# A graph network layer: 45 of its 1,563 row gathers replaced by column copies on chip, one more group of early x rows, and the node updates placed one group earlier

## The chip, the cores and the metric

The kernel runs on one core of one Trainium2 chip. A core has a matrix engine (PE, with its weight loads shown apart as PEld), a vector engine (DVE), a scalar engine (ACT), GpSimd (POOL) and a sync engine (SP) that here only issues transfers. Each engine takes its own instructions in program order and waits for the others through semaphores. The metric is the device time of one execution in microseconds (us), as the median of several runs.

## What is computed

There are 12,500 nodes with 64 features `x` and 200,000 edges with 32 features. An edge has a source and a destination; edges come sorted by destination. Every edge gives a message, messages are summed over the edges of a destination, a second small network updates the node, and the result is added to `x` and normalised over the 64 features:

```python
msg_in = concat([x[src], x[dst], edge_attr], axis=-1)        # 160 wide
messages = relu(msg_in @ mW1 + mb1) @ mW2 + mb2              # 160 -> 128 -> 64
aggregated = segment_sum(messages, dst, num_segments=12500)
upd = relu(concat([x, aggregated], axis=-1) @ uW1 + ub1) @ uW2 + ub2
out = layernorm(x + upd)
```

All data are float32.

## The kernel before

**Tables and tiles.** The first layer is linear before its relu, so the kernel computes two tables first: A = x @ (rows of `mW1` for the source) and B = x @ (rows for the destination) + `mb1`, each 12,500 x 128, both kept in device memory. Edges are worked in tiles of 128. A "group" `s` of this text is 8 tiles (`SUB`), a super group `g` is 16 tiles (`SUP`), so two groups make one super group. There are 1,563 tiles, 196 groups (the last has 3 tiles) and 98 super groups. Because the edges are sorted, the 128 destinations of a tile fall in a window of 32 nodes.

**One group.** For each group, `gather` (L147) has POOL issue one indirect transfer for each tile (L158), which brings the 128 rows of A that the sources name to one buffer of the pool `rows`. That pool has 6 buffers (`ROWB`); `frees` tells which group must be done before a buffer can be filled again. `edge_part` (L234) multiplies on PE the edge features, and a selection by destination, with a combined right side `rhs` (edge weights and the 32 window rows of B, loaded by SP in `windows`, L206), into a PSUM tile `pc`. `node_part` (L247) adds the gathered rows on DVE (L263), and ACT applies the relu (L264) into `h`. `collect` (L267) multiplies `h` on PE with a selection matrix (L276) to sum over edges by destination, into `ph`, and `aggregate` (L279) has DVE add each tile's 32 columns to `comb` (L288). The place in `comb` is read into registers first (L283), as the window's place is only known at run time.

**comb.** This is one tile of 128 partitions and two halves. Half 0 collects the hidden sums. Half 1 holds counts of edges in its first partition and, in partitions 64 to 127, the transposed `x`: column n is the feature vector of node n. `xload` brings it before the loop. `aggregate` adds to both halves at once, and what it adds in partitions 64 to 127 of half 1 is zero.

**The first groups.** While the tables are being computed (`chunk_a` on PE, ACT and DVE for A, `chunk_b` for B), the first `XG` = 7 groups don't gather from A but straight from `x`; `transpose` and a matmul in `node_part` (L257) then do the first layer for them.

**Node updates.** When the edges have moved past about 384 nodes, `columns` (L292) copies these columns of `x` to `xw` on ACT (L297), `update` and `residual` do the second network on PE (L304, L305, L315, L316) with a relu on ACT (L307), and `norm` finishes on DVE and stores the result. There are 54 such updates. Their places grow denser: from super group 62 on there is one in each super group, that is in every second group, because destinations are unevenly spread.

**Order.** The order is written out by hand in one loop over `s`, and each engine executes its part in that order: the gathers that may be issued, `norm` of an update, `windows`, `node_part(s)`, `columns`, `collect(s - 1)` and `aggregate(s - 1)`, `select` (DVE, L183 to L189), `load` and `counts` (ACT, L197) for the next super group in even groups, a part of table B in the early groups, `edge_part(s + 1)`, `update`, `residual`, and `rest`, which holds setting-up work at a few values of `s` (at group 10 it prepares the update's weights and checks the assumption about the windows). Waits between engines are set by the tiles that the instructions read and write. A tile counts as touched wherever the column is only known at run time, so everything that reads `comb` is ordered against every `aggregate`.

Of the kernel before, what the change touches and what calls it, by code (L numbers as in the profile page):

```python
# [10 lines left out]
F32 = mybir.dt.float32  # L11
I32 = mybir.dt.int32
AF = mybir.ActivationFunctionType
ALU = mybir.AluOpType
AX = mybir.AxisListType
ET = mybir.EngineType

P = 128
# [6 lines left out]
SUB = 8  # L25
# [9 lines left out]
PADWIN = 1000000  # L35
EK, SK = 0, DE
ROWB = 6
XG = 7
NCH = 8
HB = NCH // 2  # L40
EARLY = NCH * P
GE = 20
BS = 8
UB = 3
NCOL = (-(-N // P) + UB) * P
ONE = D - 1
# [15 lines left out]


@with_exitstack
def gnn_kernel(ctx: ExitStack, tc: tile.TileContext, x1T, x, eT, e_rows, src, dst, dst_row, wrow, wnext, whalf,
               mW1, mb1, mW2, mb2, uW1, ub1, uW2, ub2, out):

# [28 lines left out]

    src_s = const.tile([P, NT], I32, name="src_s")
    wint = const.tile([1, NTP], I32, name="wint")  # L100
    win0 = const.tile([1, GE * SUP], I32, name="win0")
    w1b = const.tile([P, DH], F32, name="w1b")
    b1 = const.tile([P, DH], F32, name="b1")

# [22 lines left out]
    cps = cpool.tile([P, WIN + SUP], F32, name="cps")  # L127
    slot = cps[:, :WIN]
    drc = const.tile([P, NT], F32, name="drc")
    flag_i = const.tile([1, 1], I32, name="flag_i")  # L130
    usup = const.tile([1, K], I32, name="usup")
    wh = const.tile([P, NTP // 2], I32, name="wh")
# [2 lines left out]

    rows = ctx.enter_context(tc.tile_pool(name="rows", bufs=ROWB))
    xg = {}

    def frees(s):

# [3 lines left out]
    def tiles(s):  # L144
        return range(s * SUB, min((s + 1) * SUB, NT))

    def gather(s):  # L147

        if s >= XG or s % 2 == 0:
            buf = rows.tile([P, SUB, DH], F32, name="xg")  # L150
        else:
            buf = xg[s - 1][0]
        d = DH if s >= XG else D
        a = buf.rearrange("p k (b d) -> p (k b) d", d=d)
        if s < XG:
            a = a[:, s % 2 * SUB:(s % 2 + 1) * SUB, :]
        for i, t in enumerate(tiles(s)):
            nc.gpsimd.indirect_dma_start(  # L158
                out=a[:, i, :], out_offset=None, in_=A[:, :] if s >= XG else x[:, :],
                in_offset=bass.IndirectOffsetOnAxis(ap=src_s[:, t:t + 1], axis=0))  # L160
        xg[s] = buf, a

    with tc.tile_pool(name="sup", bufs=2) as sup, tc.tile_pool(name="work", bufs=2) as work, tc.manual_schedule():
# [42 lines left out]
        def windows(g):  # L206

            nt = min(SUP, NT - g * SUP)
            r = rhs[g % 2]
            w, tab, n = (win0, B0, EARLY - WIN + 1) if g < GE else (wint, B, N)  # L210
            _, ws = nc.values_load_multi_w_load_instructions(
                w[0:1, g * SUP:g * SUP + nt], engines=[ET.SP], min_val=0, max_val=n - 1,
                skip_runtime_bounds_check_because="destinations are node numbers")
            for i in range(nt):
                q = SK + 64 * (i % 2)
                nc.sync.dma_start(r[q:q + WIN, i // 2, :], tab[bass.ds(ws[i], WIN), :])
# [17 lines left out]
        def edge_part(s):  # L234

            n = len(tiles(s))
            g, j = divmod(s, SUP // SUB)
            pc = psum.tile([P, 2, SUB // 2, DH], F32, name="pc")
            for i in range(n):
                k, b = divmod(i, 2)  # L240
                q, m = 64 * b, j * SUB // 2 + k

                nc.tensor.matmul(pc[:, b, k, :], L[g][q:q + 64, m, :], rhs[g % 2][q:q + 64, m, :],  # L243
                                 start=s >= XG or k == 0, stop=s >= XG)
            pcs[s] = pc

        def node_part(s):  # L247

            n = len(tiles(s))
            pc = pcs.pop(s)  # L250
            h = work.tile([P, 2, SUB // 2, DH], F32, name="h")
            if s < XG:
                xt = xs.pop(s)
                for i in range(n):
                    k, b = divmod(i, 2)
                    q = 64 * b
                    nc.tensor.matmul(pc[:, b, k, :], xt[q:q + 64, k, :], w1a[q:q + 64], start=False,  # L257
                                     stop=i + 2 >= n)
                nc.scalar.activation(h, pc, AF.Relu)
            else:  # L260
                a = xg.pop(s)[1].rearrange("p (k b) f -> p b k f", b=2)
                for b, m in parts(n):
                    nc.vector.tensor_tensor(h[:, b, m], pc[:, b, m], a[:, b, m], op=ALU.add)  # L263
                    nc.scalar.activation(h[:, b, m], h[:, b, m], AF.Relu)  # L264
            hs[s] = h

        def collect(s):  # L267
# [11 lines left out]
        def aggregate(s):  # L279

            n = len(tiles(s))
            ph = pht.pop(s)
            _, ws = nc.values_load_multi_w_load_instructions(  # L283
                wint[0:1, s * SUB:s * SUB + n], engines=[ET.DVE], min_val=0, max_val=N - 1,
                skip_runtime_bounds_check_because="destinations are node numbers")
            for i in range(n):
                to = comb[:, :, bass.ds(ws[i], WIN)]
                nc.vector.tensor_tensor(to, to, ph[:, i], op=ALU.add)  # L288

        us = {}  # L290

# [137 lines left out]
        for r in rhs:  # L429
            for o in (EK, EK + 64):  # L430
                nc.sync.dma_start(r[o:o + DE], mW1[2 * D:, :].unsqueeze(1).broadcast_to([DE, SUP // 2, DH]))
        relative(0, 8 * SUP)
        nc.vector.tensor_scalar(win0, wint[:, :GE * SUP], float(EARLY - WIN), None, op0=ALU.min)
        Q = NCOL // 4
        for k, c in enumerate(range(0, NB, NCH)):
            chunk_a(c)
            if k == 0:
                chunk_b(0, [B0v, Bv])
                windows(0)
            if k < 8:  # L440
                nc.vector.memset(comb[:P if k < 4 else ONE, k // 4, k % 4 * Q:(k % 4 + 1) * Q], 0.0)
            if k == 9:
                select(0)
                load(0)
                counts(0)
                for c in range(0, NCOL, XCH):
                    xload(c)
        columns_of(NCH, nc.sync)

        def rest(s):  # L450

            if s == 1:
                relative(8 * SUP, 8 * SUP + WCH)
            elif s == 2:
                relative(8 * SUP + WCH, NT)
                halves(4 * SUP, NTP // 2)
            elif s == BS:
                nc.sync.dma_start(wa, wrow.rearrange("o (p c) -> (o p) c", c=SUP))
                nc.sync.dma_start(wb, wnext.rearrange("o (p c) -> (o p) c", c=SUP))
                nc.scalar.dma_start(w2, mW2)  # L460
                nc.scalar.dma_start(u1a, uW1[D:2 * D, :])
                nc.scalar.dma_start(b2c, mb2.rearrange("(f o) -> f o", o=1))
                nc.vector.memset(uz[:D], 0.0)
                nc.vector.memset(ux[:D], 0.0)
                nc.vector.memset(eps, EPS)
                nc.vector.memset(ones, 1.0)
                nc.vector.memset(usup[:, 0:1], 0)
                nc.vector.tensor_copy(ux[D:], ident[D:, D:])
                nc.scalar.dma_start(uz[D:], uW1[0:D, :])
                nc.scalar.dma_start(ux[ONE:ONE + 1], ub2.rearrange("(o f) -> o f", o=1))  # L470
                nc.scalar.dma_start(ub1_s, ub1.rearrange("(f o) -> f o", o=1))
                nc.scalar.dma_start(u2, uW2)
            elif s == BS + 2:
                weights()
                checks()
# [14 lines left out]
        def checks():  # L490
# [30 lines left out]
            gap = work.tile([1, K + 1], F32, name="gap", bufs=1)  # L521
            nc.vector.tensor_tensor(gap[:, :K], uf[:, 1:], uf[:, :-1], op=ALU.subtract)
            nc.vector.tensor_scalar(gap[:, :K], gap[:, :K], float(UB * P - WIN), None, op0=ALU.is_gt)
            nc.vector.tensor_scalar(gap[:, K:], wint[:, GE * SUP - 1:GE * SUP], float(EARLY - WIN), None, op0=ALU.is_gt)
            bad = work.tile([1, 1], F32, name="bad", bufs=1)
            nc.vector.tensor_reduce(bad, gap, AX.X, ALU.add)
            nc.vector.tensor_tensor(flag_i, pf, bad, op=ALU.add)

        due = {SUP // SUB * (UPD[u + 1] if u + 1 < K else NSUP) + 1: u for u in range(K)}
        last = SUP // SUB * NSUP + 1
        transpose(0)
        edge_part(0)
        gathered = XG
# [1 line left out]
        for s in range(last + 3):  # L537
# [7 lines left out]
                windows(g + 1)  # L545
            if s < NSUB:
                node_part(s)
            if s in due and s < last:
                columns(due[s])
            if 1 <= s <= NSUB:  # L550
                collect(s - 1)
                aggregate(s - 1)
            if j == 0 and g + 1 < NSUP:
                select(g + 1)
                load(g + 1)
                counts(g + 1)
            if j == 1 and g + 2 < NSUP:
                loadd(g + 2)
            if chunks and s >= BS and chunks[0] < NCH + NB * (s + 1 - BS) / (SUP // SUB * (GE - 1) - BS):
                if len(chunks) > 1:  # L560
                    columns_of(chunks[1], nc.sync)
                chunk_b(chunks.pop(0), [Bv])
            if s + 1 < NSUB:
                if s + 1 < XG:
                    transpose(s + 1)
                edge_part(s + 1)
            if s == NSUB:
                columns(K - 1)
            if s in due:
                update(due[s], "pt" if s == last else "pu")  # L570
            if s - 1 in due:
# [168 lines left out]
```

## Time and profile before

| what | value |
|---|---|
| median of 3 runs | 1991.58 us (1988.15 to 1992.86) |
| time of the profiled execution | 1995.25 us |
| its span, first to last instruction | 1993.5 us |
| mean granted PE clock | 0.559 of full |
| DMA traffic | 211.74 MB, mean 106 GB/s |
| issued transfers of A rows (L158) | 1,507, and 56 of x rows |

The profile has several views. The page gives the busy time of each engine and the chain of work that ended last, followed back from the last instruction. The groups of instructions give busy time and the mean of one. The view of waits says which engine waited, at which line, for whom. The timeline gives single instructions with their start. "Issue" is idle time of an engine for which the profile shows nothing that it waits for. A name such as `xg<-tab_a,src_s` is what an instruction writes and what it reads; a `q` behind an engine's name is its sequencer, which handles register and semaphore instructions.

### The profile page before, as it was taken

The numbers are of one execution on the slowest core, as the hardware profiler recorded it, in microseconds if no ns is written. First come the engines' busy times: TensorE is split into PE (matmuls) and PEld (weight loads), VectorE is DVE, ScalarE is ACT, GpSimd is POOL, SyncE is SP. The second block draws the span as 40 slices with busy tenths as digits, with TensorE's granted clock in tenths as the row PEclk, the third lists the DMA queues.
The fourth block names the chain that finished last, engine by engine and source line by source line (L and its number), as shares of the span: only waits on it lengthen the run. The fifth ranks groups of instructions, "written<-read, shape, count | busy, mean of one in ns | idle before, by whom it ended". The sixth has DMA issues, their size and how long they took to land.

```text
span 1993.5 us, 31593 instructions
## 1 busy us (share of the span) xinstructions
PE 1364.8 (68%) x7851; PEld 1211.9 (61%) x7851; DVE 908.7 (46%) x2661; ACT 348.4 (17%) x479; POOL 1477.0 (74%) x1572
## 2 busy tenths in 40 slices
PE   3678876656566666566667766676686776776867
PEld 3577875556555666556566665665575655665756
DVE  5347544434343444444444444444454545454544
ACT  1121111111111111111111111121212121212111
POOL 7577777777777777777777777777777777777773
PEclk7665555555555555555555555556555656565555
DMA  8745554433333333333333333334333333333331
GB/s 219 217 118 151 158 139 117 115 88 100 88 99 89 99 91 99 91 97 92 99 91 94 97 100 91 97 96 102 95 99 97 96 100 98 98 98 98 98 98 39
DMA packets 244401, 211.74 MB, mean 106 GB/s; under 512 B 80542, under 2 KB 209022, under 8 KB 243824
## 3 DMA queue, kind: packets, MB, share of 16 engines
q0 software_dynamic: 50016, 100.70, 20.4%
q1 hardware_dynamic: 178644, 98.69, 17.9%
q10 hardware_dynamic: 15554, 10.31, 1.8%
q8 instruction: 63, 1.03, 0.2%
q14 instruction: 124, 1.02, 0.2%
HBM read 190.78 MB, written 18.68 MB: 105 GB/s over the span
## 4 chain that ended last, share of the span: by engine, by line
POOL 53%; issue 25%; PE 9%; DMA 8%; DVE 3%; SPq 1%; ACT 1%; DVEq 0%; ACTq 0%; POOLq 0%
POOL xg L158 53%; DMA xg<-tab_a,src_s 5%; PE ph L276 3%; DMA xl<-in_x1T 2%; PE pc L243 2%; DVE comb L288 2%; PE pu L304 1%; PE py L315 1%; DVE h L263 1%; PE pb L381 1%; PE pu L305 1%; PE py L316 1%; DMA l<-in_eT 0%; PE ph L274 0%; DVE o L333 0%
## 5 line engine op out<-in xcount | busy, mean ns | idle before, releaser
L158 POOL DMA_INDIRECT xg<-tab_a,src_s x1507 | 1423.0, 944 | 470.0 <-issue 444.2
L276 PEld LDWEIGHTS ph<-sel,h 128*128 128x128 f32 x3126 | 610.2, 299 | 34.4 <-issue 34.4
L276 PE MATMUL ph<-sel,h 128*128 128x32 f32 x3126 | 601.0, 363 | 0.0
L263 DVE TENSOR_TENSOR h<-pc,xg 128x1024 f32<-128x1024 f32 (+1 forms) x190 | 230.8, 1215 | 770.4 <-DMA xg<-tab_a,src_s 720.7
L243 PE MATMUL pc<-rhs,l 64*128 64x128 f32 x3126 | 408.9, 415 | 62.8 <-DMA l<-in_eT 24.5
L288 DVE TENSOR_TENSOR comb<-comb,ph 128x64 f32 x1563 | 345.6, 221 | 202.1 <-ACT xw L297 83.0
L243 PEld LDWEIGHTS pc<-rhs,l 64*128 64x128 f32 x3126 | 352.7, 303 | 82.8 <-DVE rs L330 30.3
L264 ACT ACTIVATE h<-h 128x1024 f32<-128x1024 f32 (+1 forms) x190 | 199.2, 1049 | 915.0 <-DVE h L263 881.7
L304 PE MATMUL pu<-comb,w2u 128*128 x108 | 88.9, 927 | 255.9 <-DVE comb L288 255.9
L274 PE MATMUL ph<-selb,one 128*128 128x256 bf16 x196 | 75.4, 384 | 239.7 <-DVE comb L288 156.8
L274 PEld LDWEIGHTS <-one 128*128 128x128 bf16 x196 | 27.3, 139 | 272.2 <-DVE comb L288 252.8
L304 PEld LDWEIGHTS pu<-comb,w2u 128*128 128x128 f32 x108 | 27.1, 312 | 271.3 <-DVE comb L288 271.3
L185 DVE TENSOR_TENSOR l<-l,cps 128x1024 f32<-128x1024 int32 (+1 forms) x101 | 123.3, 1221 | 4.8 <-DMA l<-in_dst_row 1.3
L197 ACT CAST selb<-sel 128x512 bf16<-128x512 f32 x98 | 60.4, 616 | 329.3 <-DVE sel L189 308.7
L315 PE MATMUL py<-ux,xw 128*128 128x64 f32 x324 | 87.0, 362 | 0.7 <-ACT hTu L307 0.7
L316 PE MATMUL py<-u,hTu 128*128 128x64 f32 x324 | 84.3, 354 | 0.0
L305 PE MATMUL pu<-xw,uz 128*128 128x384 f32 x108 | 80.1, 846 | 0.0
L307 ACT ACTIVATE hTu<-pu,ub_s 128x384 f32<-128x384 f32 x54 | 31.3, 580 | 270.7 <-PE pu L305 270.7
L315 PEld LDWEIGHTS py<-ux,xw 128*128 128x128 f32 x324 | 68.9, 263 | 10.8 <-issue 6.3
L316 PEld LDWEIGHTS py<-u,hTu 128*128 128x128 f32 x324 | 70.3, 268 | 0.0
L189 DVE TENSOR_TENSOR sel<-cps,drc 128x512 f32<-128x512 f32 x98 | 66.8, 682 | 0.1
L158 POOL DMA_INDIRECT xg<-in_x,src_s x56 | 53.0, 946 | 18.4 <-issue 16.5
(73 smaller groups left out, 420.2 us busy)
## 6 DMA issues: line engine op xcount, KB each, us to landing
l<-in_dst_row SPq DMA_DIRECT2D x196, 128.0 KB
l<-in_eT SPq DMA_DIRECT2D x196, 128.0 KB
rhs<-tab_b SPq DMA_DIRECT2D x1563, 16.0 KB
xg<-tab_a,src_s POOLq DMA_INDIRECT x1507
tab_b<-tb SPq DMA_DIRECT2D x13, 512.0 KB
tab_a<-tb ACTq DMA_DIRECT2D x12, 512.0 KB
out<-o SPq DMA_DIRECT2D x54, 96.0 KB
comb<-in_x1T SPq DMA_DIRECT2D x6, 520.0 KB
```

The lines of the kernel that those rows point to most:

```text
L158: nc.gpsimd.indirect_dma_start(out=a[:, i, :], out_offset=None, in_=A[:, :] if s >= XG else x[:, :], in_offset=bass.IndirectOffsetOnAxis(a ...
L185: nc.vector.tensor_tensor(l[r], l[r].bitcast(I32), node[r].unsqueeze(2).broadcast_to([r.stop - r.start, SUP // 2, P]), op=ALU.is_equal)
L243: nc.tensor.matmul(pc[:, b, k, :], L[g][q:q + 64, m, :], rhs[g % 2][q:q + 64, m, :], start=s >= XG or k == 0, stop=s >= XG)
L263: nc.vector.tensor_tensor(h[:, b, m], pc[:, b, m], a[:, b, m], op=ALU.add)
L264: nc.scalar.activation(h[:, b, m], h[:, b, m], AF.Relu)
L274: nc.tensor.matmul(ph[:, :n, 1, :], one0, SB[g][:, k0:k0 + n, :], start=True, stop=True)
L276: nc.tensor.matmul(ph[:, i, 0, :], h[:, i % 2, i // 2, :], S[g][:, k0 + i, :], start=True, stop=True)
L288: nc.vector.tensor_tensor(to, to, ph[:, i], op=ALU.add)
L304: nc.tensor.matmul(pu, w2u, comb[:, 0, bass.ds(n0, UB * P)], start=True, stop=False)
L305: nc.tensor.matmul(pu, uz, xw, start=False, stop=True)
L315: nc.tensor.matmul(py[:, i], xw[:, i * P:(i + 1) * P], ux, start=True, stop=False)
L316: nc.tensor.matmul(py[:, i], hT[:, i * P:(i + 1) * P], u2, start=False, stop=True)
```

## The change

Three things are changed.

1. In groups 15, 19, 23 and so on to 191 (one of four groups, 45 in all) the eighth tile is not gathered. Its 128 source columns are copied one by one from half 1 of `comb` to a tile `xo` of 128 columns (two such tiles take turns), and one more matmul in `edge_part` multiplies that tile with the source weights and adds it in `pc`. The copies of one tile are spread over the four iterations that come five to two groups ahead of it: in each, ACT copies 24 columns and DVE 8. The numbers of the columns are read to registers from a small table `srow`. DVE copies by adding a column of zeros that lies in PSUM. In such a group DVE's addition and ACT's relu are split, because the eighth tile has nothing to be added.
2. The first eight groups, not seven, are gathered from `x`. In the set-up the clipped copy of the windows' numbers is replaced by clipping in place, and two steps are moved: the first `windows` comes two chunks later, and the first `relative` four chunks later.
3. `columns`, `update`, `residual` and `norm` of each update come one group earlier, and `columns` stands behind `aggregate(s - 1)` in its iteration instead of ahead of it. The loop is one iteration shorter.

```diff
-XG = 7
+XG = 8
...
+CG = 4
+CF = 3 * CG
+CA = 24
+NCT = -(-(NSUB - CF) // CG)
...
+    srow = const.tile([NCT, P], I32, name="srow")
+    xo = [const.tile([P, P], F32, name=f"xo{k}") for k in range(2)]
...
+    def copied(s):
+        return s >= CF and s % CG == CG - 1 and len(tiles(s)) == SUB
...
-        for i, t in enumerate(tiles(s)):
+        for i, t in enumerate(tiles(s)[:SUB - copied(s)]):
             nc.gpsimd.indirect_dma_start(
...
+                c = copied(s) and i == n - 1
                 nc.tensor.matmul(pc[:, b, k, :], L[g][q:q + 64, m, :], rhs[g % 2][q:q + 64, m, :],
-                                 start=s >= XG or k == 0, stop=s >= XG)
+                                 start=s >= XG or k == 0, stop=s >= XG and not c)
+                if c:
+                    nc.tensor.matmul(pc[:, b, k, :], xo[s // CG % 2][q:q + 64], w1a[q:q + 64], start=False, stop=True)
...
-                for b, m in parts(n):
+                for b, m in parts(n - copied(s)):
                     nc.vector.tensor_tensor(h[:, b, m], pc[:, b, m], a[:, b, m], op=ALU.add)
                     nc.scalar.activation(h[:, b, m], h[:, b, m], AF.Relu)
+                if copied(s):
+                    nc.scalar.activation(h[:, 1, SUB // 2 - 1], pc[:, 1, SUB // 2 - 1], AF.Relu)
...
+        def copies(s):
+            t = (s + 2) // CG * CG + CG - 1
+            if t < CF or not t < NSUB or not copied(t):
+                return
+            n = P // CG
+            k = (s + 2) % CG * n
+            r = t // CG - CF // CG
+            to = xo[t // CG % 2]
+            for a, b, e, copy in ((k, k + CA, ET.Activation, nc.scalar.copy),
+                                  (k + CA, k + n, ET.DVE, lambda o, i: nc.vector.tensor_tensor(o, i, slot[D:, 0:1], op=ALU.add))):
+                _, v = nc.values_load_multi_w_load_instructions(
+                    srow[r:r + 1, a:b], engines=[e], min_val=0, max_val=N - 1,
+                    skip_runtime_bounds_check_because="sources are node numbers")
+                for i in range(a, b):
+                    copy(to[D:, i:i + 1], comb[D:, 1, bass.ds(v[i - a], 1)])
...
-        relative(0, 8 * SUP)
-        nc.vector.tensor_scalar(win0, wint[:, :GE * SUP], float(EARLY - WIN), None, op0=ALU.min)
         for k, c in enumerate(range(0, NB, NCH)):
             chunk_a(c)
             if k == 0:
                 chunk_b(0, [B0v, Bv])
+            if k == 2:
+                w0 = wint[:, :GE * SUP]
+                nc.vector.tensor_scalar(past, w0[:, GE * SUP - 1:], float(EARLY - WIN), None, op0=ALU.is_gt)
+                nc.vector.tensor_scalar(w0, w0, float(EARLY - WIN), None, op0=ALU.min)
                 windows(0)
+            if k == 4:
+                relative(0, 8 * SUP)
...
-        due = {SUP // SUB * (UPD[u + 1] if u + 1 < K else NSUP) + 1: u for u in range(K)}
-        last = SUP // SUB * NSUP + 1
+        due = {SUP // SUB * (UPD[u + 1] if u + 1 < K else NSUP): u for u in range(K)}
+        last = SUP // SUB * NSUP
...
-            if s in due and s < last:
-                columns(due[s])
             if 1 <= s <= NSUB:
                 collect(s - 1)
                 aggregate(s - 1)
+            if s in due:
+                columns(due[s])
...
                 chunk_b(chunks.pop(0), [Bv])
+            copies(s)
             if s + 1 < NSUB:
...
-            if s == NSUB:
-                columns(K - 1)
             if s in due:
                 update(due[s], "pt" if s == last else "pu")
```

More of the change, by code (lines that the diff above doesn't have):

```diff
@@ L64, in gnn_kernel @@
 @with_exitstack
-def gnn_kernel(ctx: ExitStack, tc: tile.TileContext, x1T, x, eT, e_rows, src, dst, dst_row, wrow, wnext, whalf,
+def gnn_kernel(ctx: ExitStack, tc: tile.TileContext, x1T, x, eT, e_rows, src, src_row, dst, dst_row, wrow, wnext, whalf,
                mW1, mb1, mW2, mb2, uW1, ub1, uW2, ub2, out):
@@ L100, in gnn_kernel @@
     wint = const.tile([1, NTP], I32, name="wint")
-    win0 = const.tile([1, GE * SUP], I32, name="win0")
+    past = const.tile([1, 1], F32, name="past")
     w1b = const.tile([P, DH], F32, name="w1b")
@@ L209, in windows @@
             r = rhs[g % 2]
-            w, tab, n = (win0, B0, EARLY - WIN + 1) if g < GE else (wint, B, N)
+            tab, n = (B0, EARLY - WIN + 1) if g < GE else (B, N)
             _, ws = nc.values_load_multi_w_load_instructions(
-                w[0:1, g * SUP:g * SUP + nt], engines=[ET.SP], min_val=0, max_val=n - 1,
+                wint[0:1, g * SUP:g * SUP + nt], engines=[ET.SP], min_val=0, max_val=n - 1,
                 skip_runtime_bounds_check_because="destinations are node numbers")
@@ L454, in rest @@
             elif s == 2:
+                nc.sync.dma_start(srow, src_row[CF * SUB + SUB * CG - 1::SUB * CG, :][:NCT])
                 relative(8 * SUP + WCH, NT)
@@ L523, in checks @@
             nc.vector.tensor_scalar(gap[:, :K], gap[:, :K], float(UB * P - WIN), None, op0=ALU.is_gt)
-            nc.vector.tensor_scalar(gap[:, K:], wint[:, GE * SUP - 1:GE * SUP], float(EARLY - WIN), None, op0=ALU.is_gt)
+            nc.vector.tensor_copy(gap[:, K:], past)
             bad = work.tile([1, 1], F32, name="bad", bufs=1)
@@ L722 @@
         "src": sp.reshape(-1, P).T[:, :NT],
+        "src_row": sp.reshape(-1, P),
         "dst": dp[:EPAD].reshape(-1, P).T[:, :NT],
```

## The prediction

> **What bounds the kernel now.** I read the page first (busy shares, the chain of work that ended last), then the waits, then the timeline of a stretch in the middle, of the start and of the end.
>
> ```profile
> PE 1364.8 (68%) x7851; PEld 1211.9 (61%) x7851; DVE 908.7 (46%) x2661; ACT 348.4 (17%) x479; POOL 1477.0 (74%) x1572
> POOL 53%; issue 25%; PE 9%; DMA 8%; DVE 3%; SPq 1%; ACT 1%; DVEq 0%; ACTq 0%; POOLq 0%
> L158 POOL DMA_INDIRECT xg<-tab_a,src_s x1507 | 1423.0, 944 | 470.0 <-issue 444.2
> ```
>
> The last chain is POOL's gathers and "issue", together 78%. The issue time is POOL's own: in the third line it is the idle time just before the gathers, 444.2 us. So POOL waits for nobody. The waits show who waits for POOL:
>
> ```profile
> ACT h L264 <- DVE h L263: 881.7, 180, 10.2
> DVE h L263 <- DMA xg<-tab_a,src_s: 720.7, 166, 7.1
> POOL xg L158 <- issue: 460.7, 1511, 0.3
> ```
>
> DVE waits 4.3 us on average for gathered rows, ACT waits for DVE. The timeline gives the pace:
>
> ```profile
> 1003.22 0.58 ACT L307 ACTIVATE hTu<-pu,ub_s 128x384 f32<-128x384 f32 x1 [5.06 <-PE pu L305]
> 1003.99 0.94 POOL L158 DMA_INDIRECT xg<-tab_a,src_s  x1 [0.30 <-issue]
> 1005.24 0.94 POOL L158 DMA_INDIRECT xg<-tab_a,src_s  x1 [0.30 <-issue]
> 1005.33 1.22 DVE L263 TENSOR_TENSOR h<-pc,xg 128x1024 f32<-128x1024 f32 x1 [5.13 <-DMA xg<-tab_a,src_s]
> ```
>
> From the first gather of A rows (84.04) to the last (1965.22) there are 1,506 steps: 1.249 us each, 9.99 us a group. Only one pause is long:
>
> ```profile
> 72.20 0.94 POOL L158 DMA_INDIRECT xg<-in_x,src_s  x1 [0.30 <-issue]
> 84.04 0.94 POOL L158 DMA_INDIRECT xg<-tab_a,src_s  x1 [10.90 <-DMA rhs<-tab_b]
> ```
>
> Table A isn't finished when the x rows are all issued (its last store is issued at 78.9). After the last gather (ends 1966.2) a tail of 27.3 us follows.
>
> **What the Trainium skill says.** *ScalarE: Activation LUTs*, section "What ACT_TABLE_LOAD costs": an activation without pointer operands takes 186 ns + 0.833 ns an element, and back-to-back ones overlap by about 93 ns. The trace agrees: 1057 ns for 1024 elements, 618 for 512; and in the last group a 416 ns relu is followed by the next after 323 ns. *Runtime: NRT & Kernel Launch*, section "Instruction fetch mechanics", puts a register load at about 200 ns a register even in bulk. Here the trace differs and decides: one register takes 278 ns (L294, ACT), 8 take 596 (L283, DVE), 16 take 975 (L211, SP), so some 46 ns each after the first. The same section says instructions are fetched ahead block by block, mostly hidden, which matters since ACT gets many more. *SBUF — State Buffer*, section "SBUF: two separate sides": DVE can lock GpSimd out of a shared port in two-port modes or with two SBUF inputs. DVE's copies read one SBUF operand and one in PSUM, as L288 does, and beside L288 the gathers keep their 944 ns.
>
> **Part 1, the removed gathers.** 45 x 1.249 = 56.2 us off POOL's row. A group then takes on average 7.75 x 1.249 = 9.68, a pair of groups 19.36. This is gained whole if the others keep that pace.
>
> *Cost on ACT.* Each iteration from 10 to 189 gets one load of 24 registers, 0.278 + 23 x 0.046 = 1.34 us, then 24 times a register operation and a copy of one column. No such copy is in the trace. From below: the register operation takes 46 ns (L297), single records show 40 ns until the next instruction issues and some 15 more until the one after, so 0.10 us a copy; engine overlap allows 187 - 93 = 0.094. From above: no overlap, 187 ns and the 28 ns gap of the additions at L288 (which do wait for each other), 0.215. I take c = 0.11, as these copies don't wait for each other. That makes 2.6 us of copies per group; ACT is now busy 17%.
>
> *Cost on DVE.* A load of 0.60 and 8 copies of about 0.12: 1.6 us per group, beside 9.99 us in which it is busy for some 4.6.
>
> *The new waits.* ACT's copies read `comb`, so they wait for the DVE addition before them, and the next addition waits for them. Queued behind on DVE are `select` or the next rows' addition; on ACT the next relu, for which `collect` on PE waits. The worst pair has an update: two additions to comb 4.0, `select` 2.2 (0.22 + 1.22 + 0.68), the load 1.34 (exposed after `counts`, in the other group hidden by the additions), `sd`, reciprocal and normalisation 1.3, the rows' addition 1.23, hand-overs 0.9: 11.0 + 48c. With c = 0.11 it is 16.3, below 19.36; without an update 8.0 + 5.3. So POOL stays the bound. It has six buffers, so delays of a group or two don't reach it.
>
> *Cost on PE.* The added matmul is 0.2 us in one of four groups. A pair with an update uses, at half clock (the stretch 988 to 1012 has 0.50): collect 3.9 and edge part 2.1 twice, `pu` 3.1, `py` 2.8, sum 17.9; with the extra matmul 18.0. `pu` must wait for the addition and `xw`, 2.7 us, of which the edge part covers 2.1: 18.6. Waits for `l<-in_eT` add 0.25. It fits by about 0.5 us. This is the narrowest cover in the change: if it goes, each us over costs 35 us in the dense last third.
>
> **Part 2, eight groups of x.** The extra 8 gathers (10.0 us) fill the pause of 10.9. If A is ready at the same time, A gathers still start at 84.04, with 8 tiles more behind them: -10.0 (at best -10.6, if A comes earlier since DVE no longer sits 17.6 us on `relative`). The two moved set-up steps put their 2 transfers and 16 window loads elsewhere in SP's queue, ahead of nothing that A needs; the store of A is on ACT's queue. I cost them at 0, between -3 and +3 in the start of the loop.
>
> What is late next: gather of group 17 needs the addition of group 11, which before ended at 175.0, the gather then being due at 183.8. Now it is due at 172.6. Group 11 is late because `rest(10)` holds DVE and PE. With copies on DVE (1.6) and one more x group on PE (about 1) POOL waits 5 us there; bounds 0 and 10. Later groups catch up (7 us a group from 178 to 256 before). Part 2 gives -5.
>
> **Part 3, updates one group forward.** In the middle it only shifts PE's waits (`pu` waits 255.9 us for comb now), all under POOL. At the end, PE does `pu` of the last but one update ahead of the last `collect` as before, and `norm` now precedes the last additions on DVE: followed step by step from the landing of the last rows, the last `hTu` begins 17.2 us later; before it was 16.7. So +0.5, bounds -3 and +3.
>
> **Sum.** -56.2 - 5.0 + 0.5 = -60.7. The profiled execution took 1995.25 (span 1993.5 and 1.75 around it), so it becomes 1934.5. The median of the runs is 3.7 lower: 1930.9.
>
> **Rivals.**
> *A, POOL stays the bound* (above): 1931, by its own bounds 1922 to 1938. For it: 78% of the chain, and slack of 3 us a pair on ACT and DVE.
> *B, PE becomes the bound in the last third.* For it: 18.9 of 19.36 us. Against it: in places the granted clock is full, mean 0.559. At 20.0 us a pair, 35 pairs lose 0.64 each, 22 us: 1953.
> *C, slower: the hand-over of comb between DVE and ACT becomes the bound*, in the 35 dense pairs (all their copies). Its price is c. POOL's buffers don't help, since the end is then the chain's. It decides from 11.0 + 48c = 19.36 + 60.7/35, so c = 0.21, just inside the upper bound. At c = 0.23 a pair takes 22.0, 35 x 2.7 = 94, less 60.7: 2025. For it: each copy has a register operation ahead, and nothing like it was measured. Against: at L288 the next register operation starts 13 ns after an addition has begun, so the sequencer runs ahead.
> *D, about no change*: c just below 0.21 gives it back.
>
> **How the numbers follow.** A 0.76, B 0.12, C 0.09, D 0.03. About 0.2% (4 us) is what a measurement tells from no change. Faster is A and B, 0.88; same 0.03; slower 0.09. The likeliest is 1931. The range starts at A's lower end, 1921, and goes through B's to 1953; C and D, 0.12, and the rest of B are left out.
>
> **What would show it.** Right: POOL at 1.249 us a gather with 1,518 of them, no pause near 73 us and a short one near 173; DVE still waiting for gathered rows; ACT's copies near 0.11 us apart; additions at L288's place (L304 now) starting right after the rows' addition. Wrong: POOL waiting for DVE from about 1300 us on, copies over 0.2 us apart, additions that wait for ACT by 2 us or more in each group, or PE without idle time before `pu`.

## The result, and the profile after

| | before | after |
|---|---|---|
| median, 4 runs each | 1990.30 us (1988.15 to 1992.86) | 2021.37 us (2019.32 to 2023.24) |
| profiled execution, its span | 1995.25 us, 1993.5 us | 2022.05 us, 2020.3 us |
| mean granted PE clock | 0.559 | 0.555 |
| last gather starts | 1965.22 us | 1947.23 us |
| from its end to the end of the span | 27.3 us | 72.1 us |

After is slower: the ratio is 1.0155, interval 1.0138 to 1.0173. The predicted 1931 us and its whole range are missed. The page of after, engines, chain and two groups:

```profile
PE 1436.1 (71%) x7961; PEld 1282.8 (63%) x7961; DVE 1065.8 (53%) x4146; ACT 815.3 (40%) x4890; POOL 1433.5 (71%) x1527
...
POOL 28%; PE 24%; issue 18%; DMA 10%; DVE 10%; ACT 4%; SPq 3%; ACTq 2%; DVEq 1%; POOLq 0%
...
L169 POOL DMA_INDIRECT xg<-tab_a,src_s x1454 | 1372.0, 944 | 492.9 <-issue 410.3
...
L321 ACT COPY xo<-comb 64x1 f32 x4320 | 456.6, 188 | 180.4 <-issue 109.5
```

The gathers are fewer and each is as quick as before. But POOL's share of the last chain fell from 53 to 28%, issue from 25 to 18%, and PE, DMA, DVE, ACT and SP's sequencer share the rest: no single engine sets the end. That fits a loop through several engines, which the waits have to show. Two waits of before, then those of after (us in total, times, longest):

```profile
DVE st L320 <- PE py L316: 25.9, 30, 2.6
PE pc L243 <- DMA l<-in_eT: 24.5, 29, 1.9
```

```profile
DVE h L277 <- DMA xg<-tab_a,src_s: 224.4, 68, 5.8
...
DVE st L353 <- PE py L349: 214.9, 36, 8.5
PE pc L255 <- DMA l<-in_eT: 166.3, 45, 8.3
...
POOL xg L169 <- DVE h L277: 39.4, 16, 4.4
```

DVE waited 720.7 us for gathered rows before and waits 224.4 now. Two waits that were small have grown: PE for the edge features `l<-in_eT` and DVE for `py` of an update. And POOL, which before had no wait for DVE's addition longer than the 0.3 us between any two gathers, has 14 longer ones, of 1.1 to 4.4 us; 12 of these are from 1651.8 us on. The stretches of after say when; the columns are us, then busy time and count of PE, PEld, DVE, ACT and POOL, PE clock, DMA share, GB/s:

```profile
700.00:1100.00 400.00, 287.27 (x1529) 258.44 (x1531) 211.33 (x865) 176.81 (x1117) 302.44 (x321) 0.51 0.36 97
1300.00:1600.00 300.00, 212.20 (x1119) 184.79 (x1119) 155.69 (x649) 126.84 (x768) 226.63 (x241) 0.60 0.35 95
1600.00:1900.00 300.00, 217.21 (x1154) 190.02 (x1151) 157.00 (x649) 123.85 (x742) 206.06 (x219) 0.59 0.33 89
```

Until 1600 us POOL issues 241 transfers in 300 us, as before (241 there too); then 219. PE, DVE and ACT fall back earlier: the additions to `comb` of groups 130 to 190 lie 656 us apart, 21.9 us for each of the 30 pairs, where before had 20.0. From the end of a group's last gather to its first addition it is 13 us at group 130, 46 us at group 154 and 65 us at group 172. So POOL runs ahead into its six buffers until they are full (from 1651.8 us on it pauses up to 4.4 us a pair), and the lag is paid at the end, as the long tail.

**The loop.** What takes 21.9 us is seen in SP's queue. The waits of SP before, then after:

```profile
SPq L204 <- DVE l L185: 493.0, 86, 10.0
SPq L335 <- DVE o L333: 112.1, 52, 10.1
```

```profile
SPq L368 <- DVE o L366: 477.3, 52, 12.6
SPq L215 <- DVE l L196: 133.0, 33, 8.5
```

L335 and L368 are the store of an update's result, L204 and L215 the load of edge features. SP used to wait at the load for `select`, which writes the same tile just before it; now it waits at the store, for `norm`. One turn, from the timeline of after (start, us, instruction, what ended the idle time before it):

```profile
1715.38 0.41 SPq L368 DMA_DIRECT2D out<-o  x1
...
1717.30 10.14 SPq L227 DMA_DIRECT2D rhs<-tab_b  x16
...
1727.87 0.79 SPq L215 DMA_DIRECT2D l<-in_eT  x2
...
1730.37 2.48 PE L255 MATMUL pc<-rhs,l 64*128 64x128 f32 x16 [6.74 <-DMA l<-in_eT]
...
1735.64 0.49 DVE L353 BATCH_NORM_STATS2 st<-py 128x6 f32<-128x64 f32 x3 [6.83 <-PE py L349]
...
1737.05 0.85 DVE L366 TENSOR_SCALAR o<-py,mv,rs 128x64 f32<-128x64 f32 x3
...
1737.93 0.41 SPq L368 DMA_DIRECT2D out<-o  x1
...
1739.30 0.94 POOL L169 DMA_INDIRECT xg<-tab_a,src_s  x1 [4.13 <-DVE h L277]
```

The store goes out at 1715.38; behind it SP issues the 16 window loads of the next super group, then its edge features at 1727.87; the edge part on PE waits for these; `py` of the next update (1732.78) stands behind the edge part in PE's order; `norm` needs `py`; and the next store needs `norm`, 22.55 us after the last. The written order explains why before has no such loop. There an update was due in an odd group, `norm` and store came two groups later, again odd, and between that store and the next one stood a `py` that doesn't need the loads behind the first. The timeline of before has it so:

```profile
1713.38 0.41 SPq L335 DMA_DIRECT2D out<-o  x1
...
1716.25 8.63 SPq L216 DMA_DIRECT2D rhs<-tab_b  x16
...
1727.65 0.69 PE L315 MATMUL py<-ux,xw 128*128 128x64 f32 x2
...
1729.19 0.79 SPq L204 DMA_DIRECT2D l<-in_eT  x2
...
1732.68 0.41 SPq L335 DMA_DIRECT2D out<-o  x1
```

`py` of the next store starts before the edge features behind the first store are even issued. The same loop spans two pairs of groups, and 22 us for two pairs limit nothing. With the updates a group forward the store falls in the even group, just ahead of `windows` and `load`, and `py` just behind the edge part which these feed: the loop closes within one pair.

### The profile page after: what moved, and what is told of

Its sections match the earlier page's. It is cut to its first block, busy times and chain, and to the rows that moved or that the text cites. A ratio compares the mean times of both kernels' runs of the same rounds, so it can differ in the third digit from the quotient of the medians.

```text
span 2020.3 us, 43783 instructions
## 1 busy us (share of the span) xinstructions
PE 1436.1 (71%) x7961; PEld 1282.8 (63%) x7961; DVE 1065.8 (53%) x4146; ACT 815.3 (40%) x4890; POOL 1433.5 (71%) x1527
## 4 chain that ended last, share of the span: by engine, by line
POOL 28%; PE 24%; issue 18%; DMA 10%; DVE 10%; ACT 4%; SPq 3%; ACTq 2%; DVEq 1%; POOLq 0%
POOL xg L169 28%; PE ph L292 9%; DVE comb L304 6%; PE pc L255 6%; DMA l<-in_eT 4%; DMA xg<-tab_a,src_s 4%; PE py L348 2%; ACT xo L321 2%; SPq L227 2%; PE py L349 2%; ACTq L317 1%; PE pu L337 1%; DMA xl<-in_x1T 1%; DVE sel L200 1%; DVE l L196 1%
## 5 line engine op out<-in xcount | busy, mean ns | idle before, releaser
L169 POOL DMA_INDIRECT xg<-tab_a,src_s x1454 | 1372.0, 944 | 492.9 <-issue 410.3
L255 PE MATMUL pc<-rhs,l 64*128 64x128 f32 x3126 | 435.7, 429 | 307.7 <-DMA l<-in_eT 166.3
L292 PEld LDWEIGHTS ph<-sel,h 128*128 128x128 f32 x3126 | 617.7, 302 | 23.2 <-issue 21.9
L255 PEld LDWEIGHTS pc<-rhs,l 64*128 64x128 f32 x3126 | 373.5, 316 | 333.6 <-DVE xo L316 114.7
L321 ACT COPY xo<-comb 64x1 f32 x4320 | 456.6, 188 | 180.4 <-issue 109.5
L277 DVE TENSOR_TENSOR h<-pc,xg 128x1024 f32<-128x1024 f32 (+3 forms) x234 | 226.0, 982 | 365.2 <-DMA xg<-tab_a,src_s 224.4
L278 ACT ACTIVATE h<-h 128x1024 f32<-128x1024 f32 (+3 forms) x234 | 197.2, 862 | 388.1 <-DVE h L277 295.5
L316 DVE TENSOR_TENSOR xo<-comb,cps 64x1 f32<-64x1 f32 x1440 | 156.9, 161 | 59.5 <-DVE comb L304 51.0
L353 DVE BATCH_NORM_STATS2 st<-py 128x6 f32<-128x64 f32 x162 | 26.7, 220 | 215.4 <-PE py L349 214.9
L348 PE MATMUL py<-ux,xw 128*128 128x64 f32 x324 | 103.2, 421 | 7.0 <-ACT hTu L340 7.0
L349 PE MATMUL py<-u,hTu 128*128 128x64 f32 x324 | 100.9, 414 | 0.0
L169 POOL DMA_INDIRECT xg<-in_x,src_s x64 | 60.5, 946 | 21.0 <-issue 18.9
```

Source lines behind the costliest of these rows:

```text
L169: nc.gpsimd.indirect_dma_start(out=a[:, i, :], out_offset=None, in_=A[:, :] if s >= XG else x[:, :], in_offset=bass.IndirectOffsetOnAxis(a ...
L292: nc.tensor.matmul(ph[:, i, 0, :], h[:, i % 2, i // 2, :], S[g][:, k0 + i, :], start=True, stop=True)
L316: (k + CA, k + n, ET.DVE, lambda o, i: nc.vector.tensor_tensor(o, i, slot[D:, 0:1], op=ALU.add))):
L321: copy(to[D:, i:i + 1], comb[D:, 1, bass.ds(v[i - a], 1)])
L348: nc.tensor.matmul(py[:, i], xw[:, i * P:(i + 1) * P], ux, start=True, stop=False)
L349: nc.tensor.matmul(py[:, i], hT[:, i * P:(i + 1) * P], u2, start=False, stop=True)
```

## The experiments

All ratios are to the kernel before, run beside each on the same chip (median 1991.02 us beside the first four, 1990.94 beside the last four). The question was which part loses the time, and whether it is the copies (rival C, whose 2025 us lay near the measured 2021), matrix work, or SP's queue.

**Part 3 undone.** The kernel after, with the updates at their old place:

```diff
-        due = {SUP // SUB * (UPD[u + 1] if u + 1 < K else NSUP): u for u in range(K)}
-        last = SUP // SUB * NSUP
+        due = {SUP // SUB * (UPD[u + 1] if u + 1 < K else NSUP) + 1: u for u in range(K)}
+        last = SUP // SUB * NSUP + 1
...
+            if s in due and s < last:
+                columns(due[s])
             if 1 <= s <= NSUB:
                 collect(s - 1)
                 aggregate(s - 1)
-            if s in due:
-                columns(due[s])
...
+            if s == NSUB:
+                columns(K - 1)
```

> Changed kernel with the updates at their old place (one group later, columns ahead of collect); copies, eight x groups and moved set-up steps kept. Theory SP: the update's store of its result now falls in an even iteration, ahead of the 16 window loads in SP's queue; it waits for norm, and the window loads (about 10 us to issue) and the edge features behind it start late, so that in the last third a pair of groups takes 22 us and not 19.4. Then this kernel has no such pairs: POOL stays the bound to the end, 2021 - 75 = about 1945. Rival COPIES: the copies' hand-over of comb between ACT and DVE makes the long pairs: this kernel stays above 2000. Rival PE: matrix work in the pair is too much once groups are shorter: 2000 to 2020.

Measured 1977.22 us, ratio 0.9936 [0.9920, 0.9953]. Part 3 costs 44 us beside the copies, but what is left isn't the 1945 that POOL's pace would give. This was half a miss, read below.

**The store late.** The kernel after whole; only the issue of the output's store is moved behind the window loads and the edge features of its iteration:

```diff
         def norm(u):
-            n0, py, mv, sd = us.pop(u)
+            n0, py, mv, sd = us[u]
...
-            nc.sync.dma_start(out[bass.ds(n0, UB * P), :].rearrange("(c p) d -> p c d", p=P), o)
+            us[u] = (n0, o)
+
+        def store(u):
+            n0, o = us.pop(u)
+            nc.sync.dma_start(out[bass.ds(n0, UB * P), :].rearrange("(c p) d -> p c d", p=P), o)
...
+            if s - 2 in due:
+                store(due[s - 2])
             rest(s)
```

> Changed kernel, whole, but the store of an update's result stands at the end of its iteration, behind the window loads and edge features in SP's queue. Theory SP: the long pairs go, about 1945, within 8 us of the kernel with the updates at their old place. Rival COPIES or PE: the order of the updates on PE, DVE and ACT is unchanged here, so 2010 to 2025.

Measured 1943.68 us, 0.9766 [0.9749, 0.9782]: 77.7 us less than after, by the place of one small transfer. Since the order on PE, DVE and ACT is unchanged, the rivals COPIES and PE both fall. Only the clause on the first experiment is missed: the two lie 33.5 us apart and not within 8. SP's waits of this kernel, and then DVE's for rows:

```profile
SPq L215 <- DVE l L196: 522.0, 85, 9.9
```

```profile
DVE h L277 <- DMA xg<-tab_a,src_s: 369.7, 107, 5.7
```

SP waits at the load of the edge features again, as before. Its timeline shows the new order; the update's `norm` no longer stands between SP and its loads:

```profile
1709.17 8.61 SPq L227 DMA_DIRECT2D rhs<-tab_b  x16
...
1717.34 0.85 DVE L366 TENSOR_SCALAR o<-py,mv,rs 128x64 f32<-128x64 f32 x3
...
1721.41 1.23 DVE L277 TENSOR_TENSOR h<-pc,xg 128x1024 f32<-128x1024 f32 x1 [3.22 <-DMA xg<-tab_a,src_s]
...
1725.98 0.79 SPq L215 DMA_DIRECT2D l<-in_eT  x2
...
1726.96 0.41 SPq L372 DMA_DIRECT2D out<-o  x1
```

`norm` is done at 1718.2 and its store goes at 1726.96: nobody misses those 8.8 us. From group 40 to the end the additions start 11.5 to 15 us after their group's last gather, and DVE waits for rows to the end. So all of part 1 (4,320 copies on ACT among it) fits under POOL here; the copies are not what made after slow.

**Part 3 alone.** The kernel before with `due`, `last` and `columns` as in after, no copies:

```diff
-        due = {SUP // SUB * (UPD[u + 1] if u + 1 < K else NSUP) + 1: u for u in range(K)}
-        last = SUP // SUB * NSUP + 1
+        due = {SUP // SUB * (UPD[u + 1] if u + 1 < K else NSUP): u for u in range(K)}
+        last = SUP // SUB * NSUP
...
-            if s in due and s < last:
-                columns(due[s])
...
+            if s in due:
+                columns(due[s])
...
-            if s == NSUB:
-                columns(K - 1)
```

> Kernel before with part 3 alone (updates one group forward). Theory SP: the loop store, window loads, edge features, edge part, py, norm, store doesn't need the copies; it takes about 21.9 us a pair where every pair has an update (groups 124 to 190), against 20.0 now: 33 pairs x 1.9 = 60 us slower, about 2050. Rival COPIES: without copies there is nothing to lose, 1986 to 1994.

Measured 2031.69 us, 1.0208 [1.0184, 1.0232]. The loop needs no copies: SP's waits of this kernel have the same two lines.

```profile
SPq L335 <- DVE o L333: 444.5, 52, 10.0
SPq L204 <- DVE l L185: 194.6, 34, 8.3
```

Its additions of groups 136 to 190 lie 578 us apart, 21.4 us a pair of groups. The time is shorter than the expected 2050 since the loop takes 21.4 and not 21.9 us there and the additions fall behind only from about group 140.

**Part 1 alone.** The kernel before with the copies and with the set-up steps and updates at their old places (the windows' numbers stay clipped in place); told from the kernel after, the edit of the first experiment, and

```diff
-XG = 8
+XG = 7
...
+        relative(0, 8 * SUP)
         for k, c in enumerate(range(0, NB, NCH)):
...
-            if k == 2:
+            if k == 0:
                 w0 = wint[:, :GE * SUP]
...
-            if k == 4:
-                relative(0, 8 * SUP)
```

> Kernel before with part 1 alone (one tile in four groups copied), seven x groups, old order of the set-up, old place of the updates. If the copies are hidden as forecast: 45 x 1.249 = 56 us off, 1934. Rival COPIES: 1990 or more.

Measured 1973.95 us, 0.9915 [0.9899, 0.9932]: 17 us gained where 56 are taken off POOL, between what the two gave. So with the updates at their old place the copies do cost something, in both experiments. The lines to compare are DVE's waits for `sd`, of the kernel before, of the first experiment and of the one with the late store:

```profile
DVE rs L330 <- ACT sd L324: 19.8, 54, 0.6
```

```profile
DVE rs L363 <- ACT sd L357: 151.4, 54, 3.4
```

```profile
DVE rs L363 <- ACT sd L357: 24.1, 53, 1.6
```

In the timeline of the first experiment:

```profile
1713.13 1.80 ACT L321 COPY xo<-comb 64x1 f32 x17 [1.05 <-issue]
...
1715.13 0.79 ACT L321 COPY xo<-comb 64x1 f32 x7 [0.19 <-issue]
...
1715.94 0.30 ACT L357 ACTIVATE sd<-mv,eps 128x3 f32<-128x3 f32 x1
...
1716.27 0.18 DVE L363 RECIPROCAL rs<-sd 128x3 f32<-128x3 f32 x1 [3.31 <-ACT sd L357]
```

`mv` is ready at 1713.0 and `sd` takes 0.3, but on ACT it stands behind a register load and 24 copies; the reciprocal on DVE waits 3.3 us with the next rows' addition behind it. The chain from one addition to `comb` through `pu`, `collect`, the next addition, `select`, `counts`, copies, `sd`, `norm`, the rows' addition, relu and `xw` back to an addition is 20.98 us in that pair (1719.68 to 1740.66) and 20.4 in the mean of groups 130 to 190. 30 pairs at 20.4 and not 19.36 are 31 us, and this experiment lies 33.5 above the one with the late store. SP's queue isn't the cause here: SP does wait 270.8 us at the store in the first experiment, but PE waits only 37.1 us in all for the edge features behind it, against 166.3 in after. Still, the chain through `sd` is read from the trace; no run took it away by itself. What the runs do show is that parts 3 and 1 belong together: most of the copies' gain needs the updates moved, and the store must not move with them.

**The set-up.** Four more kernels divide part 2. On a first chip the kernel before took 2803.78 us. Beside it the late store with the old set-up took 2882.47 (eight groups of `x`) and 2892.86 (seven), so 2.7 and 3.1% more than before; before with eight groups took 2799.95, and before with the moved set-up 2813.91. There a typical set of 16 window loads (the median) takes SP 20 to 23 us, against 9.0 in the other traces, and so about as long as a whole pair of groups; why isn't known. What follows is from a chip at the usual pace, on which all four were run again; that the late store pays is shown for that pace alone. The late store, with the first `relative` and `windows` back at their old places, told from the kernel after:

```diff
+        relative(0, 8 * SUP)
         for k, c in enumerate(range(0, NB, NCH)):
...
-            if k == 2:
+            if k == 0:
                 w0 = wint[:, :GE * SUP]
...
-            if k == 4:
-                relative(0, 8 * SUP)
...
+            if s - 2 in due:
+                store(due[s - 2])
             rest(s)
```

> The same kernel as e6 once more, as the kernel before took 2804 us beside that run and not 1991. Changed kernel with the late store, relative and the first window loads at their old places, eight x groups. Theory SETUP: POOL's pauses before group 20 fall from 19 us to about 8: 1944 - 10 = 1934. Rival X (the pauses come from the eighth x group and the copies): 1941 to 1946.

Measured 1940.81 us, 0.9739 [0.9723, 0.9756]: theory SETUP is missed by 7 us, and rival X fits to 0.2 us. The old places bring A's first gather forward only from 91.96 to 88.98 us, and POOL's three later pauses stay. The same with `XG = 7`:

```diff
-XG = 8
+XG = 7
```

> The same kernel as e8 once more: late store, old set-up, seven x groups. Theory SETUP: 3 us above the one with eight, about 1937. Rival X: 3 us or more below it.

Measured 1941.85 us, 0.9750 [0.9734, 0.9766]. Neither theory's order of the two is seen. They are not told apart from each other, nor by the intervals from the late store with the moved set-up (1943.68): eight groups of `x` bring nothing measurable beside the copies. Eight groups in the kernel before:

```diff
-XG = 7
+XG = 8
```

> The same kernel as e7 once more: before with eight x groups alone. Theory SETUP: 1984. Rival X: 1989 to 1993.

Measured 1987.10 us, 0.9987 [0.9977, 0.9996]: some 4 us, between what the two theories gave. The moved set-up in the kernel before, with `XG = 7` (the clipping in place goes with it; its other lines are left out here):

```diff
-        relative(0, 8 * SUP)
-        nc.vector.tensor_scalar(win0, wint[:, :GE * SUP], float(EARLY - WIN), None, op0=ALU.min)
         for k, c in enumerate(range(0, NB, NCH)):
             chunk_a(c)
...
+            if k == 2:
+                w0 = wint[:, :GE * SUP]
+                nc.vector.tensor_scalar(past, w0[:, GE * SUP - 1:], float(EARLY - WIN), None, op0=ALU.is_gt)
+                nc.vector.tensor_scalar(w0, w0, float(EARLY - WIN), None, op0=ALU.min)
                 windows(0)
+            if k == 4:
+                relative(0, 8 * SUP)
```

> The same kernel as e10 once more: before with the moved set-up steps alone, seven x groups. Theory SETUP: the pause for table A grows from 10.9 to about 19 us: 1999. Rival X: 1989 to 1993.

Measured 2004.39 us, 1.0058 [1.0041, 1.0075]: 13 us lost, in the direction of theory SETUP and 5 us beyond it. The one long pause of POOL before the first gather from A, 10.90 us in the kernel before, is here

```profile
95.01 0.94 POOL L158 DMA_INDIRECT xg<-tab_a,src_s  x1 [21.66 <-DMA rhs<-tab_b]
```

The profile names a window load as what ended this pause, as in the kernel before. The gather reads nothing that such a load brings, though, and in every trace of the usual pace with such a pause it starts 3.6 to 5.9 us after the last store of A is issued (at 91.4 here). The reason is seen in the timeline of after:

```profile
30.95 12.50 SPq L227 DMA_DIRECT2D rhs<-tab_b  x16
43.49 0.42 SPq L382 DMA_DIRECT2D drc<-in_dst  x1
44.45 0.37 SPq L383 DMA_DIRECT2D wbc<-in_wrow  x1
...
49.40 0.29 DVE L384 TENSOR_TENSOR drc<-drc,wbc 128x128 f32<-128x128 int32 x1 [12.33 <-DMA wbc<-in_wrow]
...
54.09 0.59 ACT L424 COPY tb<-pb 128x512 f32<-128x512 f32 x1 [12.76 <-DVE tb L422]
```

The transfer that `relative` needs stands behind 16 window loads in SP's queue. DVE waits 12.3 us for it with its halves of table A behind, and ACT, which copies the other halves and issues the stores of A, waits as long for DVE. In before DVE waits longer for that transfer, 17.6 us, but ahead of the first chunk of A; in after it waits behind the fifth. Up to the fifth store of A after is ahead (37.1 us against 38.9), the sixth it issues at 53.6 against 41.7, and the last at 87.8 against 78.9.

## Why the prediction was wrong, step by step

- **Part 3, "in the middle it only shifts PE's waits, all under POOL": this step failed, and it carries the miss.** It followed `pu` and the additions, and not the store which `norm` issues, though that store moves from the odd to the even iteration with it. That was to be had from the order and two rows of before: `norm` stands ahead of `windows` in the loop, and SP's 16 window loads take 8 to 10 us. With the price seen here, one turn is 1.9 (store to first window load) + 10.6 + 2.5 (edge features land) + 2.4 (edge part) + 2.9 (`py`) + 2.3 (statistics to store) = 22.6 us against 19.36. Predicted +0.5; taking the loop away gives 78.7 us between the profiled executions (2022.05 and 1943.37). Of the 90 us between the predicted and the measured median, that leaves 13; the trace puts 12 of them on part 2.
- **Part 2, "ahead of nothing that A needs": failed too, by 7.7 us.** What the moved steps are ahead of was asked of SP's queue alone, where the answer holds; but `relative` itself waits behind the window loads there, and what is queued behind `relative` on DVE is A. A's first gather starts at 91.69 in after, not at 84.04. With the eight x gathers that is -2.3 instead of -10.0.
- **Part 2, the pause near group 17.** It was put at 5 us, bounds 0 and 10. After has three pauses in its place, 2.9, 4.4 and 3.2 us, from 144 to 190 us; the late store with the old set-up has 2.4, 4.4 and 3.1, and with `XG = 7` none of the three. Only the third is at group 17; the first two are at groups 13 and 14, which the prediction passed over, and the first of them waits for PE's transposition of the added group. So one place of three was right, and the sum is at the upper bound. Part 2 as a whole gave about +7 us in the trace and not -5; between the medians with and without it, both with the late store (1943.68 and 1941.85), it is 2.
- **Part 1, right.** 1,454 gathers from A and 64 from `x`, 1.249 us apart wherever POOL doesn't pause. In the late-store kernel: -56.2 for the gathers, +7.9 for A's later start, -10.0 for eight of them moved to `x`, +8.8 for the three pauses, together -49.5; the last gather starts 50.0 us earlier than before, at 1915.22.
- **The price c, right.** 24 copies take 2.50 us, 0.101 us apart, 0.11 was taken. A load of 24 registers took 1.51 us (the middle one of 180 in after), not 1.34. Rival C had the sign and, at 2025 us, nearly the time, but by c = 0.23, which the trace denies. Part of its idea is true with the updates at their old place: there ACT's copies hold the chain through `sd`, not by their pace but by their place in ACT's queue.
- **PE's cover, right.** It was called the narrowest, at 18.9 of 19.36 us; in the late-store kernel POOL issues 241 transfers in each 300 us from 1300 on, just as before. Rival B fell.
- **The tail.** 25.4 us in the late-store kernel and 27.3 before: no loss, within the bounds given. The 72.1 us of after are the lag.
- **Small slips in the working.** A's lower bound is 1922 in one place and 1921 in another, and the three parts of `select` add up to 2.1, not 2.2. Neither changes an outcome.
- **The list of signs.** "POOL waiting for DVE from about 1300 us on" was named as a sign of being wrong, and it came, from 1651.8 on, with six buffers' delay.

The prediction named *Runtime: NRT & Kernel Launch*, "Instruction fetch mechanics", for the register load: 24 registers in 1.51 us are 63 ns each, again far below the page's 200. The gathers keep their 944 ns beside 1,440 copies on DVE, as expected. What was not drawn on would have helped: *DMA: Bandwidth & Descriptors* of the Trainium skill, "Anatomy of one DMA — SWDGE (gpsimd) path", says that a transfer's wait for a semaphore happens on the issuing sequencer before dispatch. The trace agrees for SP: its 477.3 us at L368 are such waits, and the window loads behind the store wait with it. The same page, "Issuing engines are not separate DMA queues", calls the time to initiate a transfer usually small relative to the transfer; for these window loads that is no guide, as 16 took SP 10.14 us, 0.63 each, nearly half of the turn of 22.55. How long one of them takes to land no run shows.

Left open: why the pauses from 144 to 190 us are three with the copies and one (3.9 us) with eight x groups in the kernel before, and why A's last store comes at 83.2 us with the old set-up and eight x groups beside the copies, when it comes at 76.3 with eight x groups and no copies. Single executions differ here: with the same copies, seven x groups and the set-up steps at the same places, two kernels that differ only in the updates and the store issue it at 83.5 (part 1 alone) and at 79.5 (the late store). Open too is why the copies lose on the first chip of the set-up runs.

## What to carry to other kernels

When a step moves, move its transfers with it on paper: ask where each lands in its issuing engine's queue, what it waits for there, and what is issued behind it. A store that waits for computing should stand behind the loads of the same iteration, not ahead of them. If a wait leads back to itself through several queues, count how many iterations one turn spans; here a move by one group halved that number, from two pairs of groups to one, and no busy share showed it beforehand.

## What was not expected of the hardware

- Register-addressed copies of one column are cheap on ACT: each is recorded with 188 ns, but one starts every 101 ns, its register operation included.
- A load of registers costs a first part and then little each: 278 ns for one (ACT), 596 for 8 (DVE), 975 for 16 (SP), 1509 for 24 (ACT).
- The window loads take SP 0.5 to 0.8 us each to issue (in after 16 in 8.6 to 10.3 us in the loop, 12.5 in the set-up), so a super group's set fills about half of its pair of groups; this made the store's place matter. On one chip a typical set took 20 to 23 us.
